# A state-space layer's side products: fewer ahead of the first scan, more behind it, gates ahead of inputs

## The chip, the cores and the metric

The kernel runs on one core of a Trainium2 chip: a four-layer network over two batches, in one launch. The metric is the time of one execution on the device in microseconds, the median of the runs shown.

## What is computed

Four layers, each of attention (or what stands for it) and a feed-forward part, with a layer norm behind each. The change concerns the first half of layer 2, a selective state-space block. In the kernel it has 1024 positions, 1024 features, 2048 channels and 16 states, for each of the two batches. Cut to what matters:

```python
proj = hidden_states @ in_proj_w
x, z = jnp.split(proj, 2, axis=-1)
...
xc = conv_b[None, :, None]
for k in range(K):
    xc = xc + conv_w[None, :, k:k + 1] * xp[:, :, k:k + Lq]
xc = jax.nn.silu(xc)
ssm_p = jnp.einsum('bdl,ed->ble', xc, x_proj_w)
...
dt = jax.nn.softplus(dt + dt_bias[None, :, None])
A = -jnp.exp(A_log)
...
    dA = jnp.exp(dt_t[..., None] * A)
    dBx = dt_t[..., None] * B_t[:, None, :] * x_t[..., None]
    h = dA * h + dBx
    y = jnp.einsum('bdn,bn->bd', h, C_t)
...
y = (ys + D_param[None, :, None] * xc) * jax.nn.silu(z)
return jnp.einsum('bdl,hd->blh', y, out_proj_w)
```

## The kernel before, in words

The two batches go through the whole network one after the other, so the stage of this change runs twice. It is the function l2_attn. The 1024 positions are two halves of 512 (u = 0 and 1), the 2048 channels are 16 groups of 128 (c). For each half and each group there is an x (a product of eight weight blocks, convolution, SiLU) and a z (a product of eight, SiLU).

All x of half 0 are made first (l2_in, L1367 on), then their projection to dt, B and C (l2_norm1, l2_norm, l2_spread). Then comes a loop of steps k, from -21 to 261 (L1794). Steps 0 to 255 are the scan: one step is two scans of 128 rows by 512 positions; eight steps are one channel group, 128 steps are one half. Nothing is scheduled by a tool here (manual_schedule, L1758): every engine does its instructions in the order in which the loop writes them. In one step they come in this order:

- `pick(n)` takes n *side products* off a list called `todo` (L1776). A side product is one of the eight products of an x of half 1 (`ins`, L1629 on, product at L1642), of a z (`gates`, L1685 on, product at L1697), or one of the projection of half 1 (`xproj`, L1658) or of the output (`outs`). When the list comes within a lead of 20 products of a unit, `pick` also loads that unit's weights by DMA (512 KB, L86), on SP's queue.
- `soon`: the low parts of dt go by DMA into hl (L1550).
- `rows(k + 6)`: 512 KB of dt times x are read from DRAM, spread over the states, into h (L1569, on SP's queue; nine buffers).
- `times_b(k + 2)`: GpSimd multiplies h by B (L1575).
- `keep(k - 1)`: ScalarE keeps the last state of half 0 (L1597).
- what `at(...)` put down for this step in `late`: above all the parts of dt and of x, below.
- then the first of the side products, `scan(k, 0)` on VectorE (L1589), `decay(k + 1, 1)`: a product on TensorE (L1582) and an exponential in place on ScalarE (L1584); the rest of the side products; `scan(k, 1)`; `decay(k + 2, 0)`.
- `states` (products L1609 and L1611, every second step) and `times_c(k - 1)` on VectorE (L1600).

Every eighth step from -16 on, `l2_dt` begins dt of a group: a product (L1493), then in steps k+1 to k+5 act1 to act5 on ScalarE (L1503 and L1504, L1507, L1510, L1513, L1516), in steps k+5 to k+7 three GpSimd sums (L1519, L1522, L1525), in step k+8 the product with x (L1528) and the cast to hl (L1539), in step k+9 the store of the product (dxd, L1532) and the low parts (L1544). Group 0 begins in step -16 and group 1 in step -8. In step k+4 the x of the group is read back (xi).

When the last of an x's eight products is written in step s, the rest follows by itself: in step s+1 ScalarE copies it out and begins the convolution (L1338 to L1341), in step s+2 VectorE adds three *taps* (L1346), in step s+3 ScalarE does the SiLU (L1351) and a store follows in step s+4 (xcd). When z is complete, ScalarE copies it out in the next step (L1708) and remembers it; the SiLU of all z that are remembered (L1682) is done behind the next x's SiLU. SiLU and the exponential need different tables on ScalarE, so an x's SiLU stands between two table loads (L1351 and L199). These four or more instructions are called a *block* below. y_out copies a group's sum out in steps with k % 8 = 3 (L1625).

PSUM has eight buffers of 128 by 512. All products draw from them: an x holds one from its first product until its SiLU, a decay from its product until its scan.

The order of the list, and how many products a step takes, are these lines:

```python
take(z0[:2] + x1[:6], 20)
for n in range(2, 10, 2):
    take(z0[n : n + 2] + x1[n + 4 : n + 6], 20)
take(x1[14:] + z0[10:12], 20)
...
n = 1 if -8 <= k < -1 else 3 if 0 <= k < 40 and k % 8 == 2 else 2
```

z0 and z1 are the z of the two halves, x1 the x of half 1, each a list of 16 groups. In the text, x0, x1, x2 ... are the x of half 1 by their group, and z0, z1, z2 ... the z of half 0.

Of the kernel before, what the change touches and what calls it, by code (L numbers as in the profile page):

```python
# [27 lines left out]
class Net:  # L28
# [1254 lines left out]
    def l2_attn(self, b, ready, last):  # L1283
# [4 lines left out]
        with (  # L1288
# [43 lines left out]
            def at(k, f, *args):  # L1332
                late.setdefault(k, []).append((f, args))
# [295 lines left out]
            def ins(u):  # L1629

                def one(u, c):
                    u0 = u * HALF
                    w = {}

                    def load():
                        w["w"] = self.w(i["l2_in"][c])

                    def call(k, now):
                        if k == 0:
                            w["p"] = self.ps()  # L1640
                        p = w["p"]
                        nc.tensor.matmul(  # L1642
                            p, w["w"][:, k * P : (k + 1) * P], self.xcols(k, u0, HALF), start=k == 0, stop=k == KD - 1
                        )
                        if k == KD - 1:
                            def x():
                                w["x"] = l2_x(u, c, p)
                            at(now + 1, x)
                            at(now + 2, lambda: l2_taps(c, p, w["x"]))

                            def s():
                                w["s"] = l2_silu(u, c, p, now + 3)
                                silu_z()
                            at(now + 3, s)
                    return load, [(call, k) for k in range(KD)]
                return [one(u, c) for c in range(NCH)]

            def xproj(u):  # L1658

                def one(c2):  # L1660
                    w = {}

                    def load():
                        w["x"] = self.w()
                        for n in range(2):
                            nc.sync.dma_start(w["x"][:, n * HALF : (n + 1) * HALF], xcd[u][2 * c2 + n][:])

                    def call(n, now):
                        l2_px(u, 2 * c2 + n, w["x"][:, n * HALF : (n + 1) * HALF])
                        if 2 * c2 + n == NCH - 1:  # L1670
                            for k, f in enumerate(l2_norm_steps(u)):
                                at(now + 1 + k, f)
                    return load, [(call, n) for n in range(2)]
                return [one(c2) for c2 in range(NCH // 2)]
# [10 lines left out]
            def gates(u):  # L1685

                def one(c):
                    w = {}

                    def load():  # L1690
                        w["w"] = self.w(i["l2_in"][16 + c])

                    def call(k, now):
                        if k == 0:
                            w["p"] = self.ps()
                        p = w["p"]
                        nc.tensor.matmul(  # L1697
                            p, w["w"][:, k * P : (k + 1) * P], self.xcols(k, u * HALF, HALF), start=k == 0, stop=k == KD - 1
                        )
                        if k == KD - 1:  # L1700
                            def z():
                                if c % 2 == 0:
                                    if c % 4:
                                        t = tmp("zo", 2, D)
                                    else:
                                        t = self.bp.tile([P, D], F, tag="row", name=self.nm("row"))
                                    zt[u, c], zt[u, c + 1] = t[:, :HALF], t[:, HALF:]
                                nc.scalar.copy(zt[u, c], p)  # L1708
                                raw.append((u, c))
                            at(now + 1, z)  # L1710
                            if c % 2 and u:
                                at(max(now + 2, (now + 9) // 8 * 8 - 2), silu_z)
                            elif c % 2 and c > NCH - 6:
                                at(now + 2, silu_z)

                    return load, [(call, k) for k in range(KD)]

                return [one(c) for c in range(NCH)]
# [39 lines left out]
            with self.tc.manual_schedule():  # L1758

                todo, ahead = [], []  # L1760

                def take(units, lead):
                    for n, (load, calls) in enumerate(units):
                        ahead.append((len(todo) - lead, load))
                        todo.extend(calls)

                z0, z1, x1 = gates(0), gates(1), ins(1)
                take(z0[:2] + x1[:6], 20)
                for n in range(2, 10, 2):
                    take(z0[n : n + 2] + x1[n + 4 : n + 6], 20)  # L1770
                take(x1[14:] + z0[10:12], 20)
                take(xproj(1), 9)
                take(z0[12:] + z1[:6], 20)
                taken = 0

                def pick(n):  # L1776
                    nonlocal taken
                    got = []
                    for _ in range(n):
                        while ahead and ahead[0][0] <= taken:  # L1780
                            ahead.pop(0)[1]()
                        if taken < len(todo):
                            got.append(todo[taken])
                            taken += 1
                    return got

                def first(n):
                    for f, *args in pick(n):
                        f(*args, -BEFORE)

                l2_in(0, NCH - 1, final, lambda: first(5))
                l2_px(0, NCH - 1, xo.pop())
                at(3 - BEFORE, l2_spread, 0, l2_norm(0, *l2_norm1(0, lambda: first(2))))
                for k in range(-BEFORE, 2 * SL + 6):  # L1794
                    if -16 <= k < 2 * SL - 16 and k % 8 == 0:
                        l2_dt((k + 16) // SL, (k + 16) % SL // 8, k)
                    if k == SL + 12:
                        o = outs(0)
                        for n, (a, z) in enumerate(((6, 10), (10, 12), (12, 16), (16, 16))):
                            take(o[8 * n : 8 * n + 8], 8)  # L1800
                            take(z1[a:z], 20)
                    if k == -1 or k == SL:
                        l2_cr(max(k, 0) // SL)
                    n = 1 if -8 <= k < -1 else 3 if 0 <= k < 40 and k % 8 == 2 else 2
                    batch = pick(n)

                    def pe(last=False):
                        while batch and (last or len(batch) > n - 1):
                            f, *args = batch.pop(0)
                            if f:  # L1810
                                f(*args, k)

                    live = 0 <= k < 2 * SL
                    if k in soon:
                        soon.pop(k)()
                    if 0 <= k + 6 < 2 * SL:
                        rows(k + 6)
                    if 0 <= k + 2 < 2 * SL:
                        times_b(k + 2)
                    if 0 <= k - 1 < 2 * SL:  # L1820
                        keep(k - 1)
                    for f, args in late.pop(k, []):
                        f(*args)
                    pe()
                    for m in range(2):
                        if live:
                            scan(k, m)
                        if 0 <= k + 1 + m < 2 * SL:
                            decay(k + 1 + m, 1 - m)
                        if m:  # L1830
                            break
                        pe(True)
                    if k % 2 == 1 and 0 <= k - 2 < 2 * SL:
                        states(k - 2)
                    if 0 <= k - 1 < 2 * SL:
                        times_c(k - 1)
                    if live and k % 8 == 4:
                        at(k + 7, y_out, k)
                    if 0 <= k + 2 < 2 * SL and k % 8 == 6:
                        skip((k + 2) // SL, (k + 2) % SL // 8)  # L1840
                while late:
                    for f, args in late.pop(min(late)):
                        f(*args)
# [658 lines left out]
```

## Time and profile before

| what | us |
|---|---|
| median of 3 runs (lowest, highest) | 4779.94 (4773.74, 4780.07) |
| the profiled execution, its own time | 4788.4 |
| its span, first to last instruction | 4786.6 |
| first scan of batch 0, of batch 1, from the span's start | 928.46, 3304.93 |
| step 96 of batch 0, of batch 1 | 1287.20, 3662.93 |
| end of the last scan of batch 0, of batch 1 | 1873.57, 4252.31 |
| busy over the span: TensorE, VectorE, ScalarE, GpSimd | 4429.6, 3352.5, 2037.7, 2279.8 |

The profile's lines name the engine (PE TensorE, PEld its weight loads, DVE VectorE, ACT ScalarE, POOL GpSimd, SP SyncE), the line of the kernel, the operation and its tiles, output first. A timeline's line has the start, the duration, the instruction and, in brackets, how long its engine had been idle and what released it. A product of two 32-bit operands (L1642, L1697, L1493, L1609, L1611) shows as two instructions of TensorE; the decay's (L1582) is one.

### The profile page before, as it was taken

What the parts mean: (1) busy time and instruction counts of PE and PEld (TensorE: products, weight loads), DVE (VectorE), ACT (ScalarE), POOL (GpSimd) and SP (SyncE); (2) the same over time, 40 slices, a digit from 0 to 9 for tenths busy, and PEclk for the clock granted to TensorE, in tenths of its full rate; (3) what the DMA queues carried; (4) which work ended last, traced back from release to release, by engine and by line L of the source; (5) the groups of instructions that cost most, each with busy time, mean ns of one, the idle gap of its engine ahead of it and who ended that gap; (6) DMA issues with size and microseconds to landing.
All of it is one profiled execution on the core that took longest, in us unless ns stands there. A gap on an engine that the chain in (4) does not pass through costs nothing. (4 is left out here: it accounts for less than half of the span.)

```text
span 4786.6 us, 52825 instructions
## 1 busy us (share of the span) xinstructions
PE 4429.6 (93%) x17736; PEld 2177.0 (45%) x17736; DVE 3352.5 (70%) x4564; ACT 2037.7 (43%) x4137; POOL 2279.8 (48%) x1469
## 2 busy tenths in 40 slices
PE   9989999988888888999999999999887988899999
PEld 4357655333333333564443676653332333335644
DVE  6564276499999997645365643745999999966453
ACT  2532342577766563122025223335776755631310
POOL 6732121389889995131020121304887989840310
PEclk9999999999999999999999999999999999999999
DMA  4475314588879998311111742125887899993100
GB/s 158 139 239 175 112 61 134 160 219 230 228 202 251 253 257 250 144 48 48 62 62 53 240 162 91 64 94 152 223 227 216 217 250 250 253 274 112 65 13 31
DMA packets 315507, 768.08 MB, mean 160 GB/s; under 512 B 40288, under 2 KB 112096, under 8 KB 315236
## 3 DMA queue, kind: packets, MB, share of 16 engines
q1 hardware_dynamic: 307556, 739.52, 53.4%
q0 software_dynamic: 7680, 25.17, 1.6%
q8 instruction: 142, 2.33, 0.2%
q14 instruction: 129, 1.06, 0.1%
HBM read 644.75 MB, written 100.93 MB: 156 GB/s over the span
## 5 line engine op out<-in xcount | busy, mean ns | idle before, releaser
L1575 POOL TENSOR_TENSOR h<-h,br 128x1024 f32<-128x1024 f32 x512 | 1206.2, 2370 | 113.5 <-DMA h<-dxd 66.2
L1584 ACT ACTIVATE ps<-ps,l_Alog 128x512 f32<-128x512 f32 x1024 | 663.3, 662 | 536.8 <-PE ps L1582 532.7
L1582 PE MATMUL ps<-hl,rep 128*128 128x512 f32 x1024 | 696.8, 684 | 199.2 <-DVE h L1589 194.0
L1589 DVE TENSOR_TENSOR_SCAN h<-ps,hst,h 128x512 f32<-128x512 f32 x512 | 628.5, 1267 | 10.0 <-ACT ps L1584 8.4
L1589 DVE TENSOR_TENSOR_SCAN h<-ps,h 128x512 f32<-128x512 f32 x512 | 598.1, 1207 | 22.8 <-ACT ps L1584 19.6
L1600 DVE TENSOR_TENSOR h<-h,ps 128x1024 f32<-128x1024 f32 x512 | 611.9, 1195 | 1.0 <-ACT hst L1597 1.0
L1697 PE MATMUL ps<-xT,w 128*128 128x512 f32 x1024 | 537.5, 611 | 10.1 <-DVE h L1589 10.1
L1582 PEld LDWEIGHTS ps<-hl,rep 128*128 128x128 f32 x1024 | 196.8, 193 | 657.3 <-DVE h L1589 515.4
L143 POOL TENSOR_TENSOR x<-x,row 128x1024 f32<-128x1024 f32 x80 | 190.6, 2404 | 555.9 <-PE ps L136 531.8
L960 POOL TENSOR_TENSOR s<-s,l1r 128x512 f32<-128x512 f32 x64 | 66.3, 1041 | 544.2 <-DVE l1r L959 502.0
L1611 PE MATMUL ps<-h,sel 128*32 128x512 f32 x2048 | 296.2, 628 | 8.1 <-DVE h L1600 8.1
L1519 POOL TENSOR_TENSOR e<-e,one 128x512 f32<-128x512 f32 x64 | 81.5, 1274 | 431.2 <-ACT one L1516 430.8
L1697 PEld LDWEIGHTS ps<-xT,w 128*128 128x128 f32 x1024 | 186.0, 191 | 200.1 <-issue 154.5
L1737 PE MATMUL ps<-w,w 128*128 128x512 f32 x512 | 272.2, 615 | 4.7 <-DMA w<-yd 3.1
L1642 PE MATMUL ps<-xT,w 128*128 128x512 f32 x512 | 266.3, 617 | 4.8 <-DVE h L1589 4.8
L1346 DVE SCALAR_TENSOR_TENSOR ps<-xp,l_convw,ps 128x512 f32<-128x512 f32 x192 | 145.0, 755 | 178.8 <-ACT ps L1341 174.3
L158 DVE TENSOR_TENSOR x<-x,ps 128x512 f32<-128x512 f32 x192 | 128.8, 682 | 182.9 <-PE ps L2298 136.2
L1978 PE MATMUL ps<-w,w 128*128 128x512 f32 x512 | 231.2, 599 | 0.0
L183 ACT ACTIVATE rs<-mv 128x1 f32<-128x1 f32 (+2 forms) x78 | 15.9, 204 | 505.1 <-DVE mv L177 504.9
L2292 PE MATMUL ps<-w,xT 128*128 128x512 f32 x512 | 225.9, 593 | 0.0
L110 PE MATMUL ps<-xT,w 128*128 128x512 f32 x512 | 225.1, 592 | 0.0
L373 DVE TENSOR_REDUCE mx<-ps 128x1 f32<-128x512 f32 x256 | 158.8, 683 | 40.4 <-PE ps L363 40.4
(339 smaller groups left out, 7812.0 us busy)
## 6 DMA issues: line engine op xcount, KB each, us to landing
h<-dxd SPq DMA_DIRECT2D x512, 512.0 KB
w<-l_in SPq DMA_DIRECT2D x128, 512.0 KB
w<-cvd SPq DMA_DIRECT2D x96, 512.0 KB
w<-l_out SPq DMA_DIRECT2D x96, 512.0 KB
w<-l_conv SPq DMA_DIRECT2D x48, 512.0 KB
w<-l_fw SPq DMA_DIRECT2D x32, 512.0 KB
xcd<-xo SPq DMA_DIRECT2D x64, 256.0 KB
xi<-xcd SPq DMA_DIRECT2D x64, 256.0 KB
```

The lines of the kernel that those rows point to most:

```text
L110: self.nc.tensor.matmul(out, lhsT, rhs, start=j == 0, stop=j == n - 1)
L1575: nc.gpsimd.tensor_tensor(hs[k], hs[k], norms[of(k)[0]][1].unsqueeze(1).to_broadcast([P, 2, HALF]), ALU.mult)
L1582: nc.tensor.matmul(dA[k, m], rep[:, 4 * m + q, :], hl[u, c][:, jj, :], start=True, stop=True)
L1584: nc.scalar.activation(dA[k, m], dA[k, m], AF.Exp, scale=A[:, g : g + 1])
L1589: nc.vector.tensor_tensor_scan(hs[k][:, m, :], dA.pop((k, m)), hs[k][:, m, :], hst[:, g : g + 1] if u else 0.0, ALU.mult, ALU.add)
L1600: nc.vector.tensor_tensor(hs[k], hs[k], norms[of(k)[0]][3].unsqueeze(1).to_broadcast([P, 2, HALF]), ALU.mult)
L1611: nc.tensor.matmul(py[u, c][32 * j : 32 * j + 32, :], self.sel[:, q, :], hs[k - 1 + j // 2][:, j % 2, :], start=False, stop=q == 3,)
L1642: nc.tensor.matmul(p, w["w"][:, k * P : (k + 1) * P], self.xcols(k, u0, HALF), start=k == 0, stop=k == KD - 1)
L1697: nc.tensor.matmul(p, w["w"][:, k * P : (k + 1) * P], self.xcols(k, u * HALF, HALF), start=k == 0, stop=k == KD - 1)
L1737: nc.tensor.matmul(p, y[:, cc, t * P : (t + 1) * P], wt[:, cc * HALF : (cc + 1) * HALF], start=c2 == 0 and cc == 0, stop=last,)
L1978: nc.tensor.matmul(pa[tt], y[:, cc * HALF + tt * P : cc * HALF + (tt + 1) * P], w[:, cc * HALF : (cc + 1) * HALF], start=c2 == 0 and cc == ...
L2292: nc.tensor.matmul(p, self.xcols(k, tt * P, P), wt[k][:, ns], start=k == 0, stop=False)
```

## The change

Seven steps (-15 to -9) take one side product instead of two, so that all fourteen steps from -15 to -2 take one. Seven steps (42, 50, ... 90) take three instead of two. The list begins with z0, z1 and four x instead of six, and from there on each pair of z stands ahead of the pair of x that it stood behind.

```diff
-                take(z0[:2] + x1[:6], 20)
+                take(z0[:2] + x1[:4], 20)
                 for n in range(2, 10, 2):
-                    take(z0[n : n + 2] + x1[n + 4 : n + 6], 20)
-                take(x1[14:] + z0[10:12], 20)
+                    take(z0[n : n + 2] + x1[n + 2 : n + 4], 20)
+                take(x1[12:] + z0[10:12], 20)
...
-                    n = 1 if -8 <= k < -1 else 3 if 0 <= k < 40 and k % 8 == 2 else 2
+                    n = 1 if -15 <= k < -1 else 3 if 0 <= k < 96 and k % 8 == 2 else 2
```

The list is as long as it was, and by step 96 as much of it is done. The steps of the last product of some units, as the loop writes them, before and after:

| unit | x0 | x1 | x2 | x3 | x4 | x5 | z2 | z3 | x6 | x7 | z4 | z5 | x10 | x15 | z11 |
|---|---|---|---|---|---|---|---|---|---|---|---|---|---|---|---|
| before | -13 | -9 | -2 | 2 | 6 | 10 | 13 | 17 | 21 | 25 | 28 | 32 | 52 | 80 | 88 |
| after | -11 | -3 | 2 | 5 | 17 | 20 | 9 | 13 | 32 | 35 | 24 | 28 | 62 | 81 | 88 |

The blocks of the x from x1 on stand three steps later: before in steps -6, 1, 5, 9, 13, 24, 28, 39, 43, 55, 59, 71, 75, 79 and 83, after in steps 0, 5, 8, 20, 23, 35, 38, 50, 53, 65, 69, 72, 76, 80 and 84.

## The prediction

> **What bounds the kernel now.** The page's table of costly groups gives each row's busy time, its mean in ns, and the idle time before it.
>
> ```profile
> L1589 DVE TENSOR_TENSOR_SCAN h<-ps,h 128x512 f32<-128x512 f32 x512 | 598.1, 1207 | 22.8 <-ACT ps L1584 19.6
> L1600 DVE TENSOR_TENSOR h<-h,ps 128x1024 f32<-128x1024 f32 x512 | 611.9, 1195 | 1.0 <-ACT hst L1597 1.0
> L1642 PE MATMUL ps<-xT,w 128*128 128x512 f32 x512 | 266.3, 617 | 4.8 <-DVE h L1589 4.8
> ```
>
> VectorE waits little before its scans and hardly at all before its products. So I laid the first scans of the 256 steps out by start: from step 11 on they stand 3.36 us apart, back to back (two scans and one product), and 5.60 us apart where the three taps of an x (L1346) stand between: taps cost VectorE 2.24 us. The windows view of steps 48 to 55 and 56 to 63 (columns: length, then busy time of PE, PEld, DVE, ACT, POOL) confirms it:
>
> ```profile
> 1111.61:1140.73 29.12, 24.40 (x83) 9.29 (x82) 29.05 (x29) 20.40 (x40) 28.06 (x16) 1.00 0.89 222
> 1140.73:1169.85 29.12, 26.45 (x89) 10.09 (x87) 29.05 (x28) 22.70 (x45) 24.05 (x14) 1.00 0.86 233
> ```
>
> VectorE is busy 29.05 of 29.12 us, TensorE 24.4 and 26.5: **the loop is VectorE's**, and a product there has room. Ahead of the first scan it is otherwise. The timeline of ScalarE:
>
> ```profile
> 903.28 0.63 ACT L1513 ACTIVATE lg<-one 128x512 f32<-128x512 f32 x1
> 903.82 0.18 ACT L1338 COPY xp<-hist 128x3 f32<-128x3 f32 x1
> 906.77 0.59 ACT L1339 COPY xp<-ps 128x512 f32<-128x512 f32 x1 [2.77 <-PE ps L1642]
> ...
> 908.20 0.71 ACT L1516 ACTIVATE one<-one,neg 128x512 f32<-128x512 f32 x1
> ...
> 917.16 1.28 ACT L1351 ACT_TABLE_LOAD   x1
> ...
> 922.60 0.72 ACT L1516 ACTIVATE one<-one,neg 128x512 f32<-128x512 f32 x1
> ...
> 931.77 1.04 ACT L1539 CAST hl<-lg 128x1024 fp32r<-128x1024 f32 x1 [4.44 <-POOL lg L1525]
> ```
>
> ScalarE, in order, waits 2.77 us for x0's products before the last step (L1516) of dt's chain for channel group 0, and does x1's SiLU with its two table loads (917.16 to 920.46) before group 1's. GpSimd follows it:
>
> ```profile
> 923.40 1.27 POOL L1519 TENSOR_TENSOR e<-e,one 128x512 f32<-128x512 f32 x1 [7.39 <-ACT one L1516]
> 924.63 2.36 POOL L1575 TENSOR_TENSOR h<-h,br 128x1024 f32<-128x1024 f32 x1
> ...
> 930.48 1.26 POOL L1525 TENSOR_TENSOR lg<-lg,rl 128x512 f32<-128x512 f32 x1
> ```
>
> The first row of h is multiplied (L1575) only behind group 1's L1519. Then VectorE:
>
> ```profile
> 926.21 2.34 DVE L1346 SCALAR_TENSOR_TENSOR ps<-xp,l_convw,ps 128x512 f32<-128x512 f32 x3 [7.70 <-ACT ps L1341]
> 928.46 3.45 DVE L1589 TENSOR_TENSOR_SCAN h<-ps,h 128x512 f32<-128x512 f32 x3
> 933.41 1.22 DVE L1589 TENSOR_TENSOR_SCAN h<-ps,h 128x512 f32<-128x512 f32 x1 [1.50 <-ACT ps L1584]
> ...
> 938.96 1.22 DVE L1589 TENSOR_TENSOR_SCAN h<-ps,h 128x512 f32<-128x512 f32 x1 [2.08 <-ACT ps L1584]
> ```
>
> x2's taps (926.21) stand in idle time; two waits for ScalarE's exponentials follow. From 938.96, the second scan of step 2, VectorE is the bound. Batch 1 has the same rows 2376.47 us later.
>
> **The change, part by part**, per batch, then doubled.
>
> *Products.* Weight loads of L1642 and L1697 come 0.43 us apart, two per product: 0.86 us. Seven products, 6.0 us, leave steps -15 to -9; seven come into steps 42 to 90. There, 8 steps go from 24.4 or 26.5 to 25.3 or 27.3 us of 29.1: VectorE's work hides them, cost 0. If that cover went they would cost 0.86 each.
>
> *ScalarE ahead of the scan.* I replay its queue with the rows' own spacings. x0's last product moves from step -13 to -11, so L1516 goes ahead of x0's copy: 903.9 instead of 908.20. GpSimd's three sums then end at 908.7, the cast L1539 runs at 908.85, the block of x0 (load, SiLU, two z, load: 1.35+0.5+1.15+1.29) ends at 914.1. Group 1's act1 needs L1493, which TensorE reaches at about 908.3, with nine products behind group 0's instead of sixteen. x1's last product is at step -3, its block at step 0, so none stands between: act1 1.1, act2 0.66, act3 0.81, act4 0.67 bring L1516 to 917.3 and GpSimd's L1519 to 918.1 instead of 923.40: **5.3 us earlier**.
>
> *Moved DMAs.* SP now issues x0's store (xcd) and 512 KB of z2's weights ahead of the lo halves of hl and the first row of h. The four dxd sends follow times_x (end 910.0); the store's SiLU is done at 911.7, so nothing waits there; the row is issued at 914.1 (917.50 before). Before, 512 KB issued at 917.50 had gone through by some 921, and rows followed about 2 us apart. Estimated from that, 1.5 MB from 912 on is through at 918.8; GpSimd wants it at 919.4. Cost 0; at worst 1.5, if it goes like the two 512 KB before the second row (issued 918.78, through at 925).
>
> *First steps.* x1's taps (step -1) run 919.6 to 921.8, the first scan at 921.8. But x1's block now stands in step 0, behind the cast, which waits for GpSimd's sum, 8.37 us behind L1519: 926.5. Cast 0.95, block without z 3.21, exponential 0.6: the second scan of step 1 at 931.3, after 4.9 us of waiting where there were 1.5 (933.41 before). Step 1 has no second block, so the 2.08 us wait goes: second scan of step 2 at 934.7 instead of 938.96, **-4.3** (bounds -4.3 and -2.8).
>
> *Taps.* From there on 14 sets of taps stand in VectorE's loop instead of 13, for x2's no longer hide: **+2.25**.
>
> *Blocks in the loop.* Each x's block delays the exponentials of its step. In before's rows I took the room between the end of an exponential and the start of its scan one step after each block: 1.10 us at step 80 (block alone, no z), 0.26 at 44 (with act3 and yo), 0.83 at 29 (act4), 0.74 at 6 (act5), 0.07 at 40 (with two z): two z cost 1.1 (L1682, 1.14). With the cast and two z it is negative, here on ScalarE and then VectorE:
>
> ```profile
> 1022.59 1.28 ACT L1351 ACT_TABLE_LOAD   x1
> ...
> 1024.37 1.14 ACT L1682 ACTIVATE zo<-zo 128x512 f32<-128x512 f32 x2
> 1025.53 1.28 ACT L199 ACT_TABLE_LOAD   x1
> 1026.83 1.45 ACT L1584 ACTIVATE ps<-ps,l_Alog 128x512 f32<-128x512 f32 x2
> ```
> ```profile
> 1027.52 1.22 DVE L1589 TENSOR_TENSOR_SCAN h<-ps,h 128x512 f32<-128x512 f32 x1 [0.83 <-ACT ps L1584]
> ```
>
> Before, blocks with two z fall in steps 24, 39, 55 and 71 (the last three are k%8 = 7, with no other ScalarE work). After, they fall in 20, 35, 50 and 65, beside act4, act3 with yo, act2, act1. So: 20: 0.83-1.1 = -0.27. 35: 0.26-1.1 = -0.8. 50: about 0.8-1.1 = -0.3. 65 is like step 9, whose block with act1 made VectorE wait 1.26 us (batch 0) and 1.96 (batch 1); 1.1 more, or 0.6 less where TensorE keeps its full clock: 1.8 to 3.1, I take 2.4. Blocks without z have room: at 8, 72 and 80 (cast) 1.1+0.3-0.95, at 5, 53, 69 like step 6. Waits after: 3.8 (2.3 to 5.5). Waits before, behind step 2: 3.1 and 2.5, mean 2.8. **+1.0**.
>
> *Sum:* -4.3+2.25+1.0 = -1.1 a batch, **-2.2 us** in all. From step 96 on every engine's order is the same. The profiled execution took 4788.4 us (span 4786.6, 1.8 around it): 4786.2. The median of 4779.94 is 8.5 us below that execution, so I apply the difference: **4777.7**.
>
> Two rules speak against the change. The rows show a granted clock of 1.00 in 925 to 930 and 0.66 in 930 to 935, behind 3.18 us without a matmul. The Trainium skill ("TensorE: Matmul & The Clock Gate", Part 1) halves the clock after an idle window of about 3.4 us and gives it back after a busy one: a thinner queue ahead of the scan meets it sooner. By it (an estimate) one window more would take some 1.7 us of TensorE per batch; by the rows 0 on the path, for TensorE is not on it. The Skill ("ScalarE: Activation LUTs", What ACT_TABLE_LOAD costs) adds a 1.38 us drain to each 1.28 us load, so a block would cost 2.8 more; the row disagrees (load at 912.32, next instruction at 913.61).
>
> **Rivals.**
> *A, the whole product time is won.* If products ahead of the scan were the path and all else hid, 7 x 0.86 x 2 = 12.0 us: 4767.9. For it: TensorE is busy without a gap up to the first scan. Against: act1 of group 1 ran at 916.08 only after ScalarE's earlier rows, and x2's taps must run somewhere.
> *B, the first row of h is late.* z2's weights and the store go ahead of it. If it lands only about 924, as before, the -4.3 goes: 2 x (2.25+1.0) = +6.4: 4786.3. For it: DMA is 91% to 105% busy from 917.5 to 940. Against: one 512 KB load fewer in that stretch, and a share of 0.45 or less until 917.5.
> *C, TensorE becomes the bound* in steps 42 to 90, where three products stand. The price is 0.86 each, 6.0 a batch: 2 x (6.0-1.1) = +9.8: 4789.7, slower. It decides where two such steps fall between two taps and the room, at least 1.98 us in steps 49 to 53, is used up; 1.72 leaves 0.26. Against it also: the five such steps before 40 that exist now.
> *D, the order is not what the words say.* The built order has seven products fewer ahead of the first scan; 0.02.
>
> **How the numbers follow.** Forecast and its neighbours (-5 to +4.5 us by the bounds: 2 x (-4.3+2.25+2.3-2.8) to 2 x (-2.8+2.25+5.5-2.8)) 0.74; A 0.07; B, in part or whole, 0.11; C 0.05; D and the rest 0.03. The three runs spread over 6.3 us, which widens the ends: 4769 to 4787, which leaves A and C out. About 0.2% (9.6 us) is what a measurement of this kernel can tell from no change. Faster by more: A and the edge, 0.08. Slower by more: C, and B with the upper waits, 0.06. Within: 0.86.
>
> **What would show it.** Right: L1519 of group 1 about 5 us earlier against L1493 of group 0; a first scan some 6.7 us earlier; one wait of about 5 us before the second scan of step 1 and none in step 2; 14 sets of taps behind it; waits at steps 21, 36, 51 and above all 66, none at 10 or 25; VectorE at 29.05 of 29.12 where nothing waits. Wrong: GpSimd waiting on h<-dxd before its first L1575 (B); VectorE waiting on the exponentials with TensorE, not ScalarE, late in steps 42 to 92 (C); waits at 36 and 66 near zero, or far above 3 us.

## The result and the profile after

The changed kernel took 4782.69 us (median of 13 runs, 4774.45 to 4790.52), the kernel before 4773.74 (13 runs, 4762.36 to 4780.07): ratio 1.0018, 95% interval 1.001 to 1.0025, some 8.6 us slower. The forecast was 2.2 us faster. The new median lies inside the predicted range only because the base of 4779.94 was itself 6 us above the later median of before; the change went the other way.

The profiled execution of the changed kernel took 4783.1 us (span 4781.4), *less* than that of before (4788.4). That is no contradiction, and it teaches how to compare: the layers ahead of this stage took 5.4 us less in batch 0 of that execution, and from the last scan of batch 0 to the landmark of batch 1 another 6.6 us, with the same instructions. So all that follows is measured from a *landmark*: the first instruction of L1400 in each batch, which stands just ahead of the steps (890.8 and 3267.3 us before, 885.4 and 3257.3 after).

| us from the landmark, batch 0 / batch 1 | before | after |
|---|---|---|
| first scan | 37.63 / 37.62 | 32.15 / 32.73 |
| step 3 | 50.38 / 50.37 | 47.48 / 48.07 |
| step 96 | 396.37 / 395.63 | 400.89 / 400.69 |
| steps 3 to 96 | 345.99 / 345.26 | 353.41 / 352.62 |

Step 3 comes 2.9 and 2.3 us earlier, step 96 4.5 and 5.1 us later. So 7.4 us a batch are lost between, and 9.6 us in all by step 96 agree with the 8.6 us of the timed runs. Behind step 96 the two kernels do the same work in the same order, and there the stretches 96 to 104 and 156 to 177 vary with no pattern: 46.8 to 50.6 and 75.6 to 83.8 us over the ten traces of this document. No reading of a trace here rests on them, but they are in every timed run.

The page's groups of the changed kernel, for the rows that the prediction showed of before:

```profile
L1589 DVE TENSOR_TENSOR_SCAN h<-ps,h 128x512 f32<-128x512 f32 x512 | 599.6, 1210 | 36.5 <-ACT ps L1584 27.0
L1600 DVE TENSOR_TENSOR h<-h,ps 128x1024 f32<-128x1024 f32 x512 | 620.3, 1211 | 0.2 <-ACT hst L1597 0.2
L1642 PE MATMUL ps<-xT,w 128*128 128x512 f32 x512 | 269.3, 621 | 8.9 <-DVE h L1589 8.9
```

VectorE's idle time ahead of its scans rose from 22.8 to 36.5 us, and most of it still ends with ScalarE's exponential. The windows view of the same two groups of steps, 48 to 55 and 56 to 63 (length, then busy time of PE, PEld, DVE, ACT, POOL, then the granted clock):

```profile
1100.41:1133.50 33.09, 27.86 (x88) 10.42 (x87) 31.50 (x31) 27.06 (x51) 27.76 (x16) 0.95 0.83 228
1133.50:1162.63 29.13, 27.19 (x90) 10.67 (x88) 29.06 (x28) 18.42 (x39) 26.53 (x15) 1.00 0.86 228
```

In steps 56 to 63, with three products in step 58, nothing is lost: 29.13 us, VectorE busy for 29.06, TensorE for 27.2. The third product is hidden there. In steps 48 to 55 two sets of taps stand where before there was one, and besides VectorE idles for 1.6 us. The loss is in waits, not in products.

The start, on ScalarE:

```profile
911.96 0.72 ACT L1516 ACTIVATE one<-one,neg 128x512 f32<-128x512 f32 x1
...
922.36 1.05 ACT L1539 CAST hl<-lg 128x1024 fp32r<-128x1024 f32 x1 [5.54 <-POOL lg L1525]
...
926.62 1.24 ACT L1584 ACTIVATE ps<-ps,l_Alog 128x512 f32<-128x512 f32 x2
```

on GpSimd:

```profile
912.76 1.27 POOL L1519 TENSOR_TENSOR e<-e,one 128x512 f32<-128x512 f32 x1 [6.80 <-ACT xp L1338]
915.21 2.35 POOL L1575 TENSOR_TENSOR h<-h,br 128x1024 f32<-128x1024 f32 x1 [1.17 <-DMA h<-dxd]
```

and on VectorE:

```profile
917.60 2.34 DVE L1589 TENSOR_TENSOR_SCAN h<-ps,h 128x512 f32<-128x512 f32 x2 [1.07 <-POOL h L1575]
921.13 1.22 DVE L1589 TENSOR_TENSOR_SCAN h<-ps,h 128x512 f32<-128x512 f32 x1 [1.20 <-POOL h L1575]
927.32 1.22 DVE L1589 TENSOR_TENSOR_SCAN h<-ps,h 128x512 f32<-128x512 f32 x1 [4.96 <-ACT ps L1584]
```

L1519 of group 1 stands 27.3 us behind the landmark instead of 32.6: 5.25 us earlier. Then GpSimd waits 1.17 us for the first row of h to land (1.76 in batch 1), which it did not before, and the second scan of step 1 waits 4.96 us, for ScalarE did the cast, and x1's block behind it, only when GpSimd's sum was there.

Further on there are two kinds of wait that were not foreseen. Here is the first, at x4 and x5, on ScalarE and then on VectorE:

```profile
1000.14 1.28 ACT L199 ACT_TABLE_LOAD   x1
1001.44 1.24 ACT L1584 ACTIVATE ps<-ps,l_Alog 128x512 f32<-128x512 f32 x2
...
1004.11 0.78 ACT L1341 ACTIVATE ps<-xp,l_convb,l_convw 128x512 f32<-128x512 f32 x1
```
```profile
1004.92 2.34 DVE L1346 SCALAR_TENSOR_TENSOR ps<-xp,l_convw,ps 128x512 f32<-128x512 f32 x3 [0.45 <-ACT ps L1341]
```

x4's block (with two z) ends at 1001.4 in step 20. x5's last product is written three steps behind x4's, so x5's copy is ScalarE's work in the very next step, and ScalarE, still late from the block, does not have it ready when VectorE wants the taps. Before, the second x of such a pair came four steps behind the first, and ScalarE had a step to recover.

The second kind shows in the windows of steps 89 and 90; the third column from the right is the granted clock. After:

```profile
1260.63:1263.99 3.36, 2.21 (x5) 1.06 (x4) 3.36 (x5) 2.31 (x6) 3.36 (x3) 0.66 1.07 293
1263.99:1267.35 3.36, 3.36 (x14) 0.96 (x13) 3.36 (x5) 2.46 (x4) 3.36 (x3) 0.84 1.06 242
```

and step 89 before:

```profile
1262.83:1266.19 3.36, 2.47 (x13) 0.78 (x12) 3.36 (x5) 2.90 (x7) 3.36 (x3) 1.00 1.08 312
```

TensorE loses part of its clock for some 3 us, the products and with them the exponentials slip, and VectorE waits 2.07 us (1.92 in batch 1) in step 91 instead of 0.75:

```profile
1270.64 1.22 DVE L1589 TENSOR_TENSOR_SCAN h<-ps,h 128x512 f32<-128x512 f32 x1 [2.07 <-ACT ps L1584]
```

The waits in step 9 (0.44, batch 0 only), 73 (0.81, batch 0 only) and 81 (0.62, batch 1 only) go the same way: the clock was 0.50 in step 8 and in step 72 of batch 0, and 1.00 and 0.81 in the same steps of batch 1; in steps 79 and 80 it was 0.91 and 0.58 in batch 0, 0.59 and 0.50 in batch 1. The other traces agree. Over this kernel and the variants below, a block stands in step 8, 72 or 80 of a batch 38 times. In 17 of them the clock was 0.50 over that whole step, and VectorE waited 0.40 to 0.87 us in the step behind it; in the other 21 it was 0.57 or more, and VectorE did not wait.

### The profile page after: what moved, and what is told of

Read it like the earlier page. It is cut to its first block, busy times and chain, and to the rows that moved or that the text cites. A ratio compares the mean times of both kernels' runs of the same rounds, so it can differ in the third digit from the quotient of the medians.

```text
span 4781.4 us, 52845 instructions
## 1 busy us (share of the span) xinstructions
PE 4433.3 (93%) x17736; PEld 2183.6 (46%) x17736; DVE 3357.0 (70%) x4564; ACT 2036.7 (43%) x4137; POOL 2279.2 (48%) x1469
## 5 line engine op out<-in xcount | busy, mean ns | idle before, releaser
L1582 PE MATMUL ps<-hl,rep 128*128 128x512 f32 x1024 | 715.8, 702 | 194.1 <-DVE h L1589 175.5
L1589 DVE TENSOR_TENSOR_SCAN h<-ps,h 128x512 f32<-128x512 f32 x512 | 599.6, 1210 | 36.5 <-ACT ps L1584 27.0
L1519 POOL TENSOR_TENSOR e<-e,one 128x512 f32<-128x512 f32 x64 | 81.6, 1274 | 439.4 <-ACT xp L1338 300.8
```

The source lines that it names most:

```text
L1582: nc.tensor.matmul(dA[k, m], rep[:, 4 * m + q, :], hl[u, c][:, jj, :], start=True, stop=True)
L1589: nc.vector.tensor_tensor_scan(hs[k][:, m, :], dA.pop((k, m)), hs[k][:, m, :], hst[:, g : g + 1] if u else 0.0, ALU.mult, ALU.add)
```

## The experiments

All times for stretches are batch 0 / batch 1 from the landmark. The theory: the start gains as predicted but for the late row, and the loop loses because of *where* blocks stand: which step of eight, how far behind the block the next x's copy comes, and what that does to TensorE's clock. The rivals: the third products as such (TensorE the bound), the 14th set of taps as the whole loss, and the late row of h.

**The order alone.** The new list with the old numbers of products a step:

```diff
-                    n = 1 if -15 <= k < -1 else 3 if 0 <= k < 96 and k % 8 == 2 else 2
+                    n = 1 if -8 <= k < -1 else 3 if 0 <= k < 40 and k % 8 == 2 else 2
```

> The changed list (each pair of z ahead of its pair of x) with the step counts of the kernel before: two products in steps -15 to -9, three only before step 40. The stretch from the start of the norm's square (L1400) to the first scan of step 96 took 396.4 and 395.6 us in the two batches before, 400.9 and 400.7 after. Theory S (ScalarE's blocks: what is lost is waits for exponentials and for x's copy, where a block of SiLU and table loads falls beside other ScalarE work): the start is that of before (step 3 at 50.4 us from L1400), three sets of taps hide as before, blocks with z stand in steps 16, 31, 47 and 63, the last three with k%8 = 7, where before's z blocks had 0.07 us of room; the wait at step 10 (1.3 and 2.0 us) goes, that at 25 (0.8, 0.6) moves to 17. Stretch 394 to 395.5; the whole 2 to 4 us under before. Theory O (it is the order of the list that costs): the stretch stays near 400. Theory P (TensorE: the products that stand in other steps cost, the order nothing): 396, as before.

Measured: 4768.25 us (11 runs) against 4774.55 of before (35 runs), ratio 0.9991 (0.9983 to 1.0). Step 3 at 50.38 / 50.37 as before, step 96 at 394.79 / 393.80, 1.6 and 1.8 us earlier than before. The wait in step 10 is gone; in step 17, behind x4's block with two z in step 16, there is one of 0.60 / 0.84; the blocks with two z in steps 31, 47 and 63 (k % 8 = 7) cost nothing. So the new order is not what costs time. By the traces it gains a little; the interval of the timed ratio reaches 1.0.

**z's SiLU behind the second x of a pair**, in the changed kernel: the first x of the pair gets a bare block.

```diff
-                                silu_z()
+                                if c % 2 or c == 0:
+                                    silu_z()
+                                else:
+                                    self.table()
```

> The changed kernel with one thing moved: the SiLU of the remembered z is done behind the SiLU of the second x of each pair (steps 23, 38, 53, 69) instead of the first (20, 35, 50, 65); x0 keeps its own. Theory S: waits before scans at 21, 36, 51 and 66 (0.15, 0.73, 0.13, 1.67) and before the second x's taps (0.45, 0.36, 0.94, 0.38) mostly go; about 1.3 us stay (0.6 at 66, 0.4 each behind 53 and 69). Stretch from L1400 to step 96 of 397 to 398 instead of 400.8; the whole 6 to 8 us under the changed kernel. Theory P: nothing changes, 400.8.

Measured: 4774.6 us (12 runs), ratio to before 1.0001 (0.9993 to 1.001); by the two ratios 8 us better than the changed kernel, where the traces show 5.1 us by step 96. Step 96 at 396.05 / 400.42, below and above the expected 397 to 398. The waits at 21 and 22 go and those at 36 and 37 shrink to 0.15; the one at 66 stays (1.62 / 1.97), although the block of step 65 has no z any more: the clock was 0.75 and 0.74 in steps 64 and 65 of batch 0 here, and 1.00 in both in the changed kernel, with the same 2.19 us of waiting on TensorE ahead of them. And the two batches differ by 4.4 us with the same instructions, 0.9 us of it already at step 3. Step 89 of batch 0, and of batch 1:

```profile
1256.46:1259.82 3.36, 2.21 (x13) 0.78 (x12) 3.36 (x4) 2.77 (x7) 3.36 (x3) 1.00 1.08 283
...
3637.39:3640.75 3.36, 2.21 (x5) 0.88 (x4) 3.36 (x5) 2.32 (x6) 3.36 (x3) 0.73 1.05 298
```

TensorE's waits ahead of these rows are equal, 0.62 and 1.15 us. Once the clock stays at 1.00 and step 91 waits 0.75 us, once it falls and step 91 waits 1.83. The same pattern of work can meet the lower clock or not.

The traces show what decides. In each of the ten, the changes of the recorded clock lie whole multiples of 3.413 us apart, to 1 ns, through the whole execution: the clock is set anew at the ticks of a grid that does not follow the kernel. These are the two stretches between ticks that hold the two waits in batch 0, and then, in batch 1, the one that holds both and the one behind it (columns as above):

```profile
1253.04:1256.45 3.41, 2.77 (x7) 0.81 (x5) 3.41 (x4) 2.08 (x3) 3.41 (x3) 1.00 1.04 260
1256.45:1259.87 3.42, 2.27 (x13) 0.78 (x12) 3.42 (x5) 2.83 (x7) 3.42 (x3) 1.00 1.07 282
...
3635.54:3638.95 3.41, 1.64 (x4) 0.51 (x4) 3.41 (x4) 3.41 (x7) 3.41 (x3) 1.00 1.06 333
3638.95:3642.37 3.42, 3.42 (x12) 0.81 (x10) 3.42 (x4) 1.74 (x5) 3.42 (x3) 0.50 1.05 276
```

In batch 0 a tick (1256.45) falls between the waits, TensorE is busy for 2.77 and 2.27 us, and the clock stays. In batch 1 both waits fall into one stretch, TensorE is busy for 1.64 us in it, and the next stretch has the half clock. Over steps 0 to 96 of all ten traces there are 1957 such stretches at full clock. All 94 with TensorE busy for less than 1.48 us were followed by the half clock, none of the 1810 with more than 1.86 us, and 24 of the 53 between. In the changed kernel the two waits of steps 88 and 89 lie within 2.9 us and met one stretch in both batches (busy 1.84 and 1.65 us). Before the change they lay over 4.25 us, which no stretch of 3.41 us can hold, and TensorE was busy for 2.50 us or more in each.

**z2's weights later.** The lead of z2's load cut from 20 products to 12, so that it stands behind the first rows of h on SP's queue:

```diff
-                for n in range(2, 10, 2):
+                take(z0[2:3], 12)
+                take(z0[3:4] + x1[4:6], 20)
+                for n in range(4, 10, 2):
```

> The changed kernel with the load of z2's weights (512 KB) issued in step 0 instead of step -6, so that it no longer goes ahead of the first row of h. If that load is what made GpSimd wait 1.17 us (batch 0) for the first row, the wait goes, and step 3 comes at 46.3 to 46.8 us from L1400 instead of 47.5 and 48.1; the whole 2 to 3 us less. If the row's own way through DRAM is what is late, nothing changes.

Measured: 4775.41 us (10 runs), ratio 1.0002 (0.9992 to 1.0011). GpSimd's wait that reached the first scan shrank from 1.07 / 1.64 to 0.62 / 0: step 3 at 47.04 / 46.27, where 46.3 to 46.8 was expected. VectorE in batch 1:

```profile
3291.26 2.33 DVE L1589 TENSOR_TENSOR_SCAN h<-ps,h 128x512 f32<-128x512 f32 x2
3294.73 1.23 DVE L1589 TENSOR_TENSOR_SCAN h<-ps,h 128x512 f32<-128x512 f32 x1 [1.15 <-POOL h L1575]
```

The first scan follows the taps without a wait. Over all the traces in which steps -15 to -2 take one product, the first scan waited 1.07 to 2.49 us in the twelve batches with z2's load ahead of the row, and 0.62, 0, 0 and 0 us in the four with it behind. So the load did delay the row. Half a microsecond of that is the issue of the row on SP's queue, which came 0.5 us earlier; in batch 0 that is the whole gain. By the ratios this run is 7.6 us better than the changed kernel. The traces show 1.0 us of that by step 96, since steps 3 to 96 took 353.31 / 354.00; the rest is not explained (each ratio is known to some 4 us).

**The last third product in step 92 instead of 90.**

```diff
-                    n = 1 if -15 <= k < -1 else 3 if 0 <= k < 96 and k % 8 == 2 else 2
+                    n = 1 if -15 <= k < -1 else 3 if 0 <= k < 88 and k % 8 == 2 or k == 92 else 2
```

> The changed kernel with the third product of step 90 moved to step 92. The wait at step 91, where the last z's block stands in step 90, was 0.75 us before and 2.07 and 1.92 after. If the third product makes that step's exponentials late, the wait returns to 0.75 and the stretch from L1400 to step 96 is 1.2 us shorter; if the wait comes from the granted clock or from what stands ahead, it stays near 2. The whole then moves by 2.4 us or not at all.

Measured: 4782.0 us (10 runs), ratio 1.0016 (1.0007 to 1.0025). The wait in step 91 is 2.07 / 2.07 and step 96 stands at 401.66 / 401.65: nothing gained. So the third product of step 90 is not the cause of that wait.

**x1's block ahead of the cast** of step 0:

```diff
-                            at(now + 3, s)
+                            if c == 1:
+                                late.setdefault(now + 3, []).insert(0, (s, ()))
+                            else:
+                                at(now + 3, s)
```

> The changed kernel with one move on ScalarE: in step 0 x1's SiLU with its two table loads stands ahead of the cast of group 1, not behind it. In the changed kernel ScalarE is idle for 5.54 us ahead of that cast, and the second scan of step 1 waits 4.96 us for the exponential behind the block. Theory (the block of 3.2 us without z is what stands behind the cast): the block falls into the idle time, the wait of 4.96 shrinks to about 1.8, and step 3 begins 44.3 to 45 us after the landmark instead of 47.5 and 48.1; steps 3 to 96 are as in the changed kernel, 352.5 to 353.5. Rival (the cast is late whatever stands behind it, and VectorE then waits for TensorE or GpSimd): step 3 stays above 47.

Measured, in a single run (4791.26 us, a time that says nothing on an effect of this size): the wait of 4.96 us became 1.64 in both batches, step 3 came at 45.29 / 44.46, steps 3 to 96 took 353.5 in both. The theory holds. GpSimd's wait for the first row reached the first scan with 2.20 / 1.37 us here, which is why batch 0 lies 0.3 us above the expected 44.3 to 45.

**The last blocks one step earlier**, by moving two of the steps with three products:

```diff
-                    n = 1 if -15 <= k < -1 else 3 if 0 <= k < 96 and k % 8 == 2 else 2
+                    n = 1 if -15 <= k < -1 else 3 if 0 <= k < 72 and k % 8 == 2 or k in (74, 76, 82) else 2
```

> The changed kernel with two of the steps of three products moved: 74 and 76 take them instead of 74 and 90, so that the block of x14 stands in step 79 and that of x15 in step 83, as before the change, instead of 80 and 84. Theory (the block in step 84 stands ahead of the last part of dt's chain, the cast of step 88 comes 1.0 us later, TensorE idles in steps 88 and 89 and its granted clock falls to 0.50 in steps 89 and 90): the cast comes 0.3 us after step 88 instead of 1.3, the granted clock stays at 1.00, the wait at step 91 is 0.75 us instead of 1.9 to 2.07, and the wait at 81 (0.62 in batch 1) goes: steps 3 to 96 take 351 to 352.3 us instead of 353.4 and 352.6. Rival (the wait at 91 comes from what stands in front of it in the list, the third products): it stays at 1.9 or more.

Measured, in a single run: steps 3 to 96 took 351.77 / 351.55. The cast of step 88 starts 0.22 us behind that step's first scan instead of 1.26 and ends 1.04 us earlier, and step 89 and VectorE's wait in step 91 are as before the change:

```profile
1260.61:1263.97 3.36, 2.47 (x13) 0.78 (x12) 3.36 (x5) 2.89 (x7) 3.36 (x3) 1.00 1.08 302
```
```profile
1269.29 1.22 DVE L1589 TENSOR_TENSOR_SCAN h<-ps,h 128x512 f32<-128x512 f32 x1 [0.75 <-ACT ps L1584]
```

It is 0.76 us in batch 1. A new wait of 0.88 us stands in step 78 of batch 0: there x14's copy is behind x13's block, the first kind again. So the chain is: x15's block in step 84 delays the last parts of dt (L1516 comes 9.2 us ahead of step 88, and 10.2 before the change), with them GpSimd's sums, the cast and two exponentials; TensorE then waits 0.62 and 1.15 us where before it waited 0.88 and 0.89, its clock drops in step 89, for the reason shown above, and VectorE waits in step 91.

**The catch-up early.** The twelve steps with three products put into steps 5 to 34, so that from x6 on the blocks stand where the order alone had put them, while steps -15 to -2 still take one product:

```diff
-                    n = 1 if -15 <= k < -1 else 3 if 0 <= k < 96 and k % 8 == 2 else 2
+                    n = 1 if -15 <= k < -1 else 3 if 9 <= k < 28 and k % 2 or k in (5, 34) else 2
```

> The changed kernel with the twelve steps of three products put earlier (5, the odd steps from 9 to 27, and 34), so that from x6 on every block stands where the order alone put it with the old numbers of products: with two z in steps 31, 47 and 63 (k % 8 = 7), without z in 35, 51, 67, 71, 75, 79 and 83, and the second x of a pair four steps behind the first. What stays of the change: one product a step from step -15 to -2. Theory (blocks in the wrong steps and pairs three steps apart cost the changed kernel its time): the waits at 21, 22, 36, 37, 49, 51, 52, 66, 73 or 81 go and that at 91 falls to 0.75: steps 3 to 96 take 345.5 to 347.5 us instead of 353, step 96 comes at 393 to 395.5 after the landmark, and both batches together are 10 to 14 us below the changed kernel, ratio to before 0.998 to 0.9995. Rival (TensorE becomes the bound where every second step takes three products, 0.86 us each for ten of them): 3 to 8.6 us of it are given back between steps 9 and 28, and step 96 comes at 397 or later.

Measured: 4776.83 us (11 runs) against 4772.55 (21 runs), ratio 1.0003 (0.9993 to 1.0013). Steps 3 to 96 took 347.32 / 347.08, 6.1 and 5.5 us less than in the changed kernel, with no wait between step 19 and step 91; step 96 came at 395.17 / 395.69. The start is as in the changed kernel, so the waits were due to the blocks' places. The rival does not show either: in steps 8 to 15 TensorE was busy for the whole 26.9 us, and VectorE too. The two waits left ahead of step 91 stand at x4: its copy is queued behind the cast of step 16, which waits for GpSimd,

```profile
980.84 1.04 ACT L1539 CAST hl<-lg 128x1024 fp32r<-128x1024 f32 x1 [0.91 <-POOL lg L1525]
...
982.59 0.78 ACT L1341 ACTIVATE ps<-xp,l_convb,l_convw 128x512 f32<-128x512 f32 x1
```

and the taps wait 1.28 / 1.40 us; the block in step 18 costs 0.8. The time is above what I expected: by the ratios some 7 us below the changed kernel instead of 10 to 14. In the traces step 96 comes 5.7 / 5.0 us earlier than there, 10.7 in all, though the row of h cost 1.45 / 2.19 us at the start of this execution instead of 1.07 / 1.64; the difference to the timed runs lies within their intervals, of some 4 us each.

**All of it together**: the early catch-up, x1's block ahead of the cast, z2's weights later.

> The early steps of three products, with two more edits: x1's SiLU ahead of the cast of step 0, and z2's weights loaded eight products later, so that they no longer stand ahead of the first row of h. If each part gives what it should by itself (start: step 3 at 43.5 to 45 us instead of 47.5 and 48.1; steps 3 to 96 345.5 to 347.5), step 96 comes at 389 to 392.5 us after the landmark, 3.5 to 7 us a batch ahead of the kernel before, and the median lies 7 to 14 us below it: ratio 0.997 to 0.9985. Rival (what VectorE gains at the start meets GpSimd's products or the rows of h, which then are late in steps 3 to 10): step 96 at 393 or later.

Measured: 4764.34 us (11 runs), ratio 0.9982 (0.9973 to 0.9991), some 8.6 us below before and faster than all others here. First scan at 30.99 / 31.00, step 3 at 42.99 / 42.96, step 96 at 391.58 / 390.18, all as expected or better; only steps 3 to 96 of batch 0 took longer (348.59, with a wait of 0.83 us in step 9 behind a clock of 0.50). On VectorE the first scan waits for nothing and the wait for x1's block is a third of what it was:

```profile
919.99 2.33 DVE L1589 TENSOR_TENSOR_SCAN h<-ps,h 128x512 f32<-128x512 f32 x2
923.51 1.23 DVE L1589 TENSOR_TENSOR_SCAN h<-ps,h 128x512 f32<-128x512 f32 x1 [1.20 <-POOL h L1575]
926.37 1.22 DVE L1589 TENSOR_TENSOR_SCAN h<-ps,h 128x512 f32<-128x512 f32 x1 [1.63 <-ACT ps L1584]
```

The start gain of fewer products was there to be had: 7.4 us a batch, not 2.3 to 2.9, once the loop and the queues were arranged for it.

## Why the prediction was wrong

*What held.* VectorE is the bound of the loop, products in it are hidden (steps 56 to 63; the step 92 variant; the early catch-up). L1519 of group 1 came 5.25 us earlier (5.3 predicted), the wait in step 1 was 4.96 us (4.9), the waits in steps 2, 10 and 25 went. Taps: taking the waits off steps 3 to 96 leaves 342.2 / 342.0 us before and 344.6 / 344.2 in the last experiment, which has 14 sets there as well: 2.4 and 2.3 us more, against +2.25. Rival C, the one that was slower, was right in sign and wrong in mechanism.

*The step that failed: "Blocks in the loop", +1.0.* The waits between steps 3 and 96 sum to 8.1 / 7.5 us, and to 3.8 / 3.3 before: +4.3 and +4.2. (The prediction's 3.1 and 2.5 for before leave out 0.75 us in step 91, which it took to be the same after.) The list has three parts.

- The waits that were priced, in steps 21, 36, 51 and 66: 2.7 / 2.6 us (0.15, 0.72, 0.13 and 1.67 in batch 0), against 3.8 predicted (0.27, 0.8, 0.3 and 2.4). The room worked out from the rows of before was good to a few tenths, and 66 came a little under its lower bound of 1.8. This part was priced too high, not too low.
- Taps that wait for an x's copy, in steps 22, 37, 49 and 52: 0.45, 0.36, 0.38 and 0.94, 2.1 us, priced at nothing. I had only asked what a block does to the exponentials of its own step. The table in the change shows x4 and x5 at 17 and 20 where before all later pairs were four apart, and I did not ask what the second x's copy, one step behind the block, would find. (Step 49 is a variant: x8's copy, in step 48, stands behind that step's cast, which waits for GpSimd, as x4's does in the early catch-up.)
- Waits that come from a lower granted clock, in steps 9, 73 or 81, and 91: 3.3 / 2.5 us where before had 0.75, in step 91 alone. I had written that the lower clock costs 0 on the path, since TensorE is not on it. That is true of a product's length, not of its end: where ScalarE has just been late, the decay's product is next in the chain, and its delay reaches VectorE. Here the Trainium skill ("TensorE: Matmul & The Clock Gate", Part 1, What's actually happening) says that activity is judged over a window that runs freely and does not start with the work. The second experiment agrees: on its grid of 3.413 us the same work met 1.00 once and 0.73 once. I had used the rule only for the start, and only for a stretch without any product.

Another 0.9 us a batch is what remains (7.4, less 2.25 for the taps and 4.2 for the waits). VectorE's busy time in steps 3 to 96 does grow by 3.05 us in both batches, 0.8 more than the taps. It is probably spread over the waits, behind each of which the two scans of a step lose their usual overlap of 0.1 us; no run isolates it.

*The term that was mis-sized: start, -4.3.* It was -2.9 / -2.3. "Cost 0; at worst 1.5" for the first row of h was wrong at its best value: issued when predicted (908.84, 23.4 us behind the landmark; predicted 23.3), GpSimd could use it 6.4 us later instead of the estimated 4.7, and the first scan came at 32.15 / 32.73 instead of 31.0. The second batch's -2.3 is outside the bounds (-4.3 to -2.8). With z2's load out of the way and x1's block moved, it came at 30.99 / 31.00, so the rest of that replay was right. The doubt I named as rival B was real, at a third to a half of its price of 4.3 a batch.

In sum, the forecast of -1.1 a batch became +4.5 / +5.1: the start lost 1.4 / 2.0, the taps nothing, and the loop 4.2 / 4.1 with what remains. (The upper neighbour that the prediction gives as +4.5 us is +4.3 by its own terms; nothing rests on it.)

What stays open: which of the stretches with TensorE busy for 1.5 to 1.85 us lower the clock and which do not; why batch 0 of the run with z2's weights later still waited 0.62 us for the row; and why z2's weights later gained 6.6 us more in the timed runs than in its trace. The new numbers of products with the old order were not tried, for there z2's SiLU would come behind y_out, which takes z2.

## What to carry to other kernels

Shifting a queue by three steps re-times everything that hangs on it: list the step of every follow-up instruction before and after, and ask for each what stands ahead of it on its engine, the next unit's copy as well as the scan of the same step. An engine with spare time still matters through the *end* of its product; a change that moves two of its waits closer together can cost it its clock and then the path, even if the waits grow no longer in sum. And a small gain found at the start should be paid for at once, close by: the twelve third products placed within 30 steps instead of 90 turned +8.6 us into no change, and with two queue moves into -8.6.

## What the runs showed of the hardware

- TensorE's granted clock fell with no long idle stretch: in steps 88 and 89 TensorE was busy for 2.71 and 2.21 of 3.36 us each, its longest wait was 1.15 us, and the clock over step 89 was 0.66. Before, with 2.47 us busy in each of the two, it stayed at 1.00. The sum over the two steps is the same; what differs is how much of the waiting falls between two ticks of the clock's own grid of 3.413 us. Busy for 1.64 to 1.84 us of such a stretch there, it got the half clock in the next one, in nine batches of nine; busy for 2.27 us or more, it kept the full one. The Trainium skill ("TensorE: Matmul & The Clock Gate", Part 1, What's actually happening) gives the half clock to an idle window of about 3.4 us. The rows agree with its length, but the window need not be idle: 1.84 us of work in it did not keep the clock.
- A load of 512 KB queued on SP ahead of the row of h made the first scan wait 1.07 to 2.49 us (twelve batches), against 0 to 0.62 without it (four batches), though the load's own issue took 0.46 us.
- Behind a table load (1.28 us) ScalarE lost no time: the next instruction started 0.01 us later in 62 of 64 loads before the change and in 63 of 68 after it, from just ahead of the first scan to step 96.
